# Layer 0: all three projections in one set of seven block products

## The chip, the cores and the metric

The kernel runs on one core of a Trainium2 chip. The metric is device time in microseconds (us) of one execution. The kernel before took 2167.6 us (median of three runs, 2166.02 to 2168.73). The profile is of one further execution.

The engines go by their profile names: PE (TensorE, matrix products), PEld (its weight loads), DVE (VectorE), ACT (ScalarE), POOL (GpSimd) and SP (SyncE, here only a queue that issues transfers). Lines such as L554 are lines of the kernel before; where a line of the changed kernel is meant, the text says so.

## The reference, cut to what matters

Two layers run on 4 x 512 tokens of width 512. Each layer adds an attention and a mixture of experts to its input. Only the attention of layer 0 is touched:

```python
xn = _layernorm(x)
q  = apply_rope(rmsnorm((xn @ Wq  + bq ).heads(16, 128), qn_w), pos)
lk = apply_rope(rmsnorm((xn @ Wlk + blk).heads(16, 128), kn_w), pos)
lv = (xn @ Wlv + blv).heads(16, 128)
ck = apply_rope(rmsnorm(entries @ Wk + bk, kn_w), block_ends)
cv = entries @ Wv + bv
ctx_sparse = top-8 attention of q over (ck, cv)
ctx_local  = windowed softmax attention of q over (lk, lv)
out = (0.5 * (ctx_sparse + ctx_local)) @ Wo + bo
```

`entries` are tokens averaged by fours with softmax weights. `rmsnorm` divides by the root of the mean square over the 128 elements of a head. `apply_rope` turns the first 64 of the 128 elements of a head and leaves the other 64 as they are. The scores of a query and a key are a sum over all 128 elements, so a factor on one of the 128 positions may sit on either side.

## The kernel before, in words

**Steps.** Layer 0 handles two heads (one group `g`) and one sequence of 512 tokens (`b`) at a time: 8 groups by 4 sequences are 32 steps. In step `i` the attention of step `i` is interleaved with the projections of step `i+1`; the projections of step 0 stand in the setup ahead of the loop. Other work (routing, experts, the sums of their results, the norm of the next layer) hangs on the places `run0((i, 0..4))` of each step. The two experts of a step are gathered, transposed (L382), multiplied (`apply`, L392: four products of 512 columns) and evicted by DVE (L394). A scheduler then orders the instructions of each engine. Each engine runs its own list in order.

**Projections.** A matmul takes 128 tokens as weights and streams the columns of a weight matrix, 256 for two heads. The queries are plain: for each half `t` of the sequence (256 tokens), `queries0(t)` does 2 x 4 matmuls of 256 columns into one PSUM bank (L554). Keys and values together use Winograd's form of Strassen's 2 x 2 block product: the tokens are cut into two halves, the width of 512 into two halves, and the columns into "keys" and "values"; seven block products `p1` to `p7` (L524) replace eight. Each is 2 x 2 matmuls of 256 columns into one bank. A step so has 16 + 28 = 44 matmuls of 256 columns. DVE forms sums of the input blocks (`sums_x`, L516 to L518, and L571), sums of the weights once per group (`combine_weights`, L102 to L106), and adds the products up as it evicts them (L561 to L587).

**After the projection.** `finish` and `rope` take the rows of two heads and two token blocks, four head rows of 128: ACT sums their squares (L432), POOL adds a constant and takes the power -0.5 (L434 to L437), DVE applies the rotation with tables `t1`, `t2` (L440 to L443), ACT scales the queries by the norm (L447). The keys stay unscaled; their norm enters as `scale` of the exponential (L613). Four PE transposes and one ACT copy (L543, L544) put a half of the queries or keys into `qkT`. The norm weights `qn_w` and `kn_w` are folded into the tables, which are 128 wide: cosine 1 in the unrotated half.

**Attention.** `scores(i, h)` does the sparse scores (L600), DVE's selection of eight (L603 to L625), the local scores (L609), exponentials (L613) and POOL's masks (L617). `turn` transposes the sparse weights (L635, L637), `context` multiplies with the values (L651 to L657), divides and adds the two halves (L660 to L670: ACT scales the sparse part into a tile `half`, DVE adds the local part). `turn_context` transposes (L677, L678), `output` multiplies with `Wo` (L685: eight products of 512 columns) and DVE adds to `acc` (L688).

**PSUM.** Layer 0 has 8 banks: 3 of tag "mm" (products, experts, output), 3 of "sc" (scores, context), 2 of "tr" (transposes). A bank is free again when DVE or ACT has read it.

**Setup.** SP issues the loads in the order x block 0, Wq, three bias broadcasts, x block 1, Wlk, the norm weights, cosine and sine tables, x blocks 2 and 3, Wlv, and the rest. `layernorm` (L199 to L211) runs on DVE, POOL (power), PE (transposes) and ACT (copy to `xnT`). `tables` (L176 to L195) builds the tables on POOL, ahead of the norms of blocks 2 and 3.

## Time and profile before

| what | value |
|---|---|
| median of three runs | 2167.6 us |
| the profiled execution | 2168.7 us, its span from first to last instruction 2166.8 us |
| PE busy | 2108.3 us, 97% of the span |
| DVE, ACT, POOL busy | 1458.9, 848.4, 687.0 us |
| granted PE clock, mean | 0.993 of full |
| PE idle in 0 to 54 us | 54.00 - 37.08 = 16.9 us |
| PE idle in 500 to 1000 us | 0.0 us |
| first sparse scores of step 0 | start at 61.16 us |
| a step between 520 and 990 us | 46.98 us (520.95, 567.93, 614.91 ... for the starts of L685) |

Busy time is the share in which an engine works on an instruction. PE's matmuls are pipelined: one of 256 columns has a duration of 0.38 us, but eight of them start and end within 3.46 us, 0.4325 us each. So costs on PE are taken from the starts in the order of time, not from the mean durations. Idle time is put down to what ended it.

### The profile page before, as it was taken

Reading aid. Unit: us, or ns where it says so; the run is one execution under the profiler, and the core shown is the slowest. Engines: PE = TensorE matmul, PEld = TensorE weight load, DVE = VectorE, ACT = ScalarE, POOL = GpSimd, SP = SyncE. Lnnn points to the kernel's source line nnn. Section 1 sums busy time; section 2 is a strip of 40 time slices with the busy share of each in tenths; the row PEclk is TensorE's granted clock in tenths of the full one; section 3 lists DMA queues with packets and bytes.
Section 4 is the critical chain, followed back from the end, with each engine's and each line's share of the span. In section 5 each row is a group of like instructions: output and inputs, shape, how many; then the busy total and the mean of one; then the engine's idle time right before and its main releaser. Section 6 shows DMA issues by size and latency. Waiting matters only on the chain.

```text
span 2166.8 us, 28936 instructions
## 1 busy us (share of the span) xinstructions
PE 2108.3 (97%) x9970; PEld 1392.0 (64%) x9970; DVE 1458.9 (67%) x3674; ACT 848.4 (39%) x2649; POOL 687.0 (32%) x725
## 2 busy tenths in 40 slices
PE   6999999999999999999999999999999999999998
PEld 5667877777777777777777887885334343443332
DVE  6868976666666766666666788885485444446775
ACT  3444444334444334444433444552333233333332
POOL 3212234343323323333323444443012222213430
PEclk9999999999999999999999999999999999999998
DMA  7001023322322332232232112102016566653321
GB/s 229 35 11 38 11 73 97 106 78 83 105 98 74 105 105 71 83 124 80 78 123 83 59 50 63 35 30 92 10 69 209 203 227 209 205 198 117 107 83 41
DMA packets 70813, 211.24 MB, mean 97 GB/s; under 512 B 8449, under 2 KB 25857, under 8 KB 60673
## 3 DMA queue, kind: packets, MB, share of 16 engines
q0 software_dynamic: 22592, 139.47, 19.2%
q1 hardware_dynamic: 45760, 65.63, 9.4%
q10 hardware_dynamic: 2304, 4.20, 0.5%
q8 instruction: 81, 1.33, 0.3%
q14 instruction: 76, 0.61, 0.1%
HBM read 176.24 MB, written 33.03 MB: 97 GB/s over the span
## 4 chain that ended last, share of the span: by engine, by line
PE 68%; issue 13%; DVE 8%; POOL 5%; DMA 3%; ACT 3%; SPq 0%; POOLq 0%; ACTq 0%; DVEq 0%
PE p L524 15%; PE pq L554 9%; PE op L685 9%; PE hp_r L392 7%; PE st L609 4%; PE sp L600 2%; PE trq L543 2%; PE qp L905 2%; POOL we_r L375 2%; PE ca L653 2%; PE o L976 1%; DVE pS L936 1%; PE st L916 1%; DMA row_r<-yd,slot_r 1%; PE cc L657 1%
## 5 line engine op out<-in xcount | busy, mean ns | idle before, releaser
L392 PE MATMUL hp_r<-we_r,xT_r 128*128 128x512 f32 x624 | 283.4, 597 | 4.3 <-DMA we_r<-in_ewx,wrow_r 4.2
L617 POOL TENSOR_TENSOR lT<-lT,lmask 128x512 f32<-128x512 f32 (+1 forms) x128 | 151.2, 1196 | 318.6 <-ACT lT L613 318.6
L554 PE MATMUL pq<-Wq,xnT 128*128 128x256 f32 x1024 | 234.0, 381 | 1.2 <-DVE u L570 1.2
L685 PE MATMUL op<-Wo,cT 128*128 128x512 f32 x512 | 230.5, 599 | 2.1 <-DVE lv L587 2.1
L554 PEld LDWEIGHTS pq<-Wq,xnT 128*128 128x128 f32 x1024 | 190.2, 191 | 24.9 <-DVE u L570 1.5
L392 PEld LDWEIGHTS hp_r<-we_r,xT_r 128*128 128x128 f32 x624 | 115.1, 191 | 139.4 <-issue 129.6
L373 POOL DMA_INDIRECT xr_r<-xnd,rows_r x78 | 83.6, 1072 | 330.9 <-PE trm_r L382 232.9
L613 ACT ACTIVATE lT<-st,ss 128x256 f32<-128x256 f32 (+1 forms) x256 | 96.8, 443 | 234.2 <-PE st L609 234.1
L544 ACT COPY qkT<-trq 128x512 f32<-128x512 f32 x128 | 74.7, 583 | 231.6 <-PE trq L543 231.2
L685 PEld LDWEIGHTS op<-Wo,cT 128*128 128x128 f32 x512 | 91.7, 190 | 113.8 <-issue 82.3
L918 ACT ACTIVATE pT<-st 128x1024 f32<-128x1024 f32 x128 | 123.8, 1019 | 70.1 <-PE st L916 54.5
L437 POOL TENSOR_TENSOR ss<-ss,nhalf 128x4 f32<-128x4 f32 x128 | 144.5, 1129 | 10.7
L384 ACT COPY xT_r<-trm_r 128x512 f32<-128x512 f32 x78 | 45.2, 580 | 260.6 <-PE trm_r L382 203.0
L688 DVE TENSOR_TENSOR acc<-acc,op 128x512 f32<-128x512 f32 x128 | 87.5, 684 | 80.7 <-PE op L685 80.5
L394 DVE TENSOR_TENSOR yr_r<-hp_r,we_r 128x512 f32<-128x512 f32 x78 | 53.7, 688 | 116.5 <-PE hp_r L392 116.5
L447 ACT ACTIVATE r<-r,ss 128x128 f32<-128x128 f32 x256 | 81.9, 390 | 105.8 <-POOL ss L437 103.4
L524 PE MATMUL p<-Wlv,x 128*128 128x256 f32 x512 | 117.5, 380 | 0.0
L524 PE MATMUL p<-Wlk,xnT 128*128 128x256 f32 x512 | 117.4, 383 | 0.0
L524 PE MATMUL p<-wT,x 128*128 128x256 f32 x512 | 117.4, 380 | 0.0
L407 POOL DMA_INDIRECT row_r<-yd,slot_r x64 | 75.3, 1176 | 120.1 <-DVE row_r L1008 53.6
L524 PEld LDWEIGHTS p<-wT,x 128*128 128x128 f32 x512 | 95.9, 190 | 23.8 <-issue 12.1
L524 PEld LDWEIGHTS p<-Wlv,x 128*128 128x128 f32 x512 | 95.5, 190 | 20.7 <-issue 9.1
(253 smaller groups left out, 4394.4 us busy)
## 6 DMA issues: line engine op xcount, KB each, us to landing
yd<-yr_r SPq DMA_DIRECT2D x78, 256.0 KB, 2.4
acc<-in_x SPq DMA_DIRECT2D x16, 256.0 KB, 5.1
Wq<-in_Wq SPq DMA_DIRECT2D x8, 512.0 KB, 3.7
Wlk<-in_Wlk SPq DMA_DIRECT2D x8, 512.0 KB, 3.6
xnd<-xn ACTq DMA_DIRECT2D x16, 256.0 KB, 2.6
Wlv<-in_Wlv SPq DMA_DIRECT2D x8, 512.0 KB, 9.1
Wo<-in_Wo SPq DMA_DIRECT2D x8, 512.0 KB, 3.6
xnd<-xn SPq DMA_DIRECT2D x16, 256.0 KB, 2.0
```

The lines of the kernel that those rows point to most:

```text
L373: G.indirect_dma_start(out=x, out_offset=None, in_=xnd, in_offset=at_rows(self.r.rows[:, i : i + 1]))
L392: PE.matmul(hp, lhsT=xT[:, k, :], rhs=w[:, ts(k, HID)], start=(k == 0), stop=(k == KC - 1))
L437: G.tensor_tensor(ss, ss, nhalf[:, 0:n], ALU.pow)
L447: A.activation(r1[:, h, :], r1[:, h, :], AF.Copy, scale=ss[:, h : h + 1])
L524: PE.matmul(p[:, c, :], lhsT=x[:, k, ts(c, P)], rhs=w[:, k, :], start=(k == 0), stop=(k == 1))
L554: PE.matmul(pq[:, c, :], lhsT=xnT[:, k, ds(b * S + (2 * t + c) * P, P)], rhs=w_q[:, k, :], start=(k == 0), stop=(k == KC - 1))
L609: PE.matmul(st[:, ds((t % 2) * 256, n)], lhsT=qkT[:, HG + h, ts(t, P)], rhs=qkT[:, h, ds(t * P, n)], start=True, stop=True)
L613: A.activation(lT[:, ds(half * 512 + c * 256, n)], st[:, ds(c * 256, n)], AF.Exp, scale=norm_k[(i, half)][:, c * HG + h : c * HG + h + 1])
L617: G.tensor_tensor(dst, dst, lmask.rearrange("p a w j -> p (a w j)")[:, 0:n], ALU.mult)
L685: PE.matmul(op, lhsT=cT[:, h, ts(t, P)], rhs=wo[:, h, :], start=(h == 0), stop=(h == HG - 1))
L688: V.tensor_tensor(acc[:, n, :], acc[:, n, :], op, ALU.add)
L918: A.activation(pt[:, ts(pair, 2), :], st, AF.Exp, scale=SCALE1)
```

## The change

It has these parts.

1. **Queries in the products.** The columns of a group are regrouped by the host into two matrices of 384: `wA` holds the two query heads and the key of head 0, `wB` the two value heads and the key of head 1. The seven products now run over these two column halves, 2 x 2 matmuls of 384 columns each, and yield queries, keys and values. The products of 16 matmuls for the queries (L554) are gone. A bank holds one token block: 14 evictions of 384 columns instead of 2 + 7 of 512.
2. **Sums of x.** They are formed only in the projections of steps 0 to 3 (now four sums, the fourth also at that place), written to a DRAM tile `xsd`, and loaded again for the same sequence in steps 4 to 31 (four loads of 256 KB each).
3. **Rotation.** Only the 64 rotated columns are touched, in place. The factor of the unrotated 64 positions is one column `turned`, applied by ACT as it copies the transposed keys. Squares run over six head rows (two query heads and one key head, two token blocks) and once over four (the second key head, inside `lv`).
4. **Order.** The products are spread: the first four ahead of the scores of head 1, `second(0)` and the query transposes ahead of the context of head 0, `second(1)` after it, `third` after the turn of head 1, `fourth`, the other query transposes, the keys of head 0 and `fifth` between the context of head 1 and the output. The keys of head 1 are transposed in the next step, after the scores of head 0. `qkT` has one buffer instead of two.
5. **Half sums in place.** ACT writes the sparse half into the context tile itself, and DVE adds to it there; the tile `half` is gone.
6. **Setup.** All four x blocks of the first sequence and the norm weights are loaded first, then `wA` and `wB` in two parts each with the tables between. The tables are 64 wide, and are built behind the first four norms. The norms of blocks 0 and 1 are kept in program order on DVE.

The diff, cut to its core:

```diff
-        for nm in ("Wq", "Wlk", "Wlv"):
-            w = wpool.tile([P, KC, HG * D], F32, tag=nm, name=f"{nm}_{g}")
+        for i, nm in enumerate(("wA", "wB")):
+            w = wpool.tile([P, KC, 3 * D], F32, tag=nm, name=f"{nm}_{g}")
...
-        t2_, t3_, t4_ = (wpool.tile([P, 2, HG * D], ...) for x in (2, 3, 4))
+        t2_, t3_, t4_ = (wpool.tile([P, 2, 3 * D], ...) for x in (2, 3, 4))
+        for o, x, y in ((t3_, b2_, b1), (b1, b1, w_a[:, 0:2, :]), (t2_, b2_, b1), (t4_, t2_, a2),
+                        (b2[:, 1, :], b2[:, 1, :], b2[:, 0, :])):
...
+    for n in range(TC):
+        load_x(n)
...
+    def load_sums(i):
+        for n in range(4):
+            xs[n] = wk0.tile([P, 2, 256], F32, tag=f"x{n}", name=f"x{n}_{i}", bufs=1)
+            if i >= B:
+                nc.sync.dma_start(out=xs[n].rearrange("p k t -> p (k t)"), in_=xsd[steps[i][1], n])
...
-        qkT = qp.tile([P, 2 * HG, S], F32, tag="qkT", name=f"qkT_{g}_{b}")
+        qkT = qp.tile([P, 2 * HG, S], F32, tag="qkT", name=f"qkT_{g}_{b}", bufs=1)
...
+        def product(nm, x, w, c):
+            p = psum("mm", f"{nm}_{i}_{c}")[:, 0 : 3 * D]
+            for k in range(2):
+                PE.matmul(p, lhsT=x[:, k, ts(c, P)], rhs=w[:, k, :], start=(k == 0), stop=(k == 1))
+            return p
...
+        def finish(t):
+            x = qb[t].rearrange("p c (h d) -> p (c h) d", d=D)
+            sq[t] = squares(x, 6, wk0, f"{i}_{t}", float(D))
+            by = lambda tt: tt[:, ts(t, 2), :, :].rearrange("p c h d -> p (c h) d")
+            rotate(x, by(t1), by(t2), 6, wk0, f"{i}_{t}")
+            for j in (0, 1, 3, 4):
+                A.activation(x[:, j, :], x[:, j, :], AF.Copy, scale=sq[t][:, j : j + 1])
...
+        def turn_keys(h):
+            tr = psum("tr", f"trk_{i}_{h}")
+            for t in range(TC):
+                PE.transpose(tr[:, ts(t, P)], lv[:, t, 2, 0:D] if h else qb[t // 2][:, t % 2, ts(2, D)], ident)
+            A.activation(qkT[:, HG + h, :], tr, AF.Copy, scale=turned[:, 0:1])
+        def first():
+        def second(c):
+        def third():
+        def fourth():
+        def fifth():
...
-            A.activation(half[:, t, :], spa[t][:, 0:D], AF.Copy, scale=sums[:, at : at + 1])
+            A.activation(ctx_[:, t, :], spa[t][:, 0:D], AF.Copy, scale=sums[:, at : at + 1])
...
         em0, lT0 = scores(i, 0, now)
+        turn_last(1)
+        if more:
+            load_sums(i + 1)
+            qkT, sums_x, first, second, third, fourth, fifth, turn_queries, turn_keys = project(i + 1)
+            first()
+            sums_x()
         run0((i, 0))
         em1, lT1 = scores(i, 1, now)
         sT0 = turn(i, 0, em0)
         run0((i, 1))
-        back_k1 = keys_b(back_q0)
-        back_k0()
+            second(0)
+            turn_queries(0)
         ctx0 = context(i, 0, lT0, sT0, lv)
+            second(1)
         sT1 = turn(i, 1, em1)
-        back_q1 = queries_b()
+            third()
         run0((i, 2))
-        back_k1()
         ctx1 = context(i, 1, lT1, sT1, lv)
         turn_context(i, 0, ctx0, cT)
         run0((i, 3))
-        values_()
-        back_q1()
+            fourth()
+            turn_queries(1)
+            turn_keys(0)
+            fifth()
         turn_context(i, 1, ctx1, cT)
         for t in range(TC):
             output(i, t, cT)
```

## The prediction

> **What bounds the kernel now.** First the page's busy times and slices, then the chain that ended last, then the costliest groups, and for prices one step in order of time.

> ```profile
> PE 2108.3 (97%) x9970; PEld 1392.0 (64%) x9970; DVE 1458.9 (67%) x3674; ACT 848.4 (39%) x2649; POOL 687.0 (32%) x725
> PE   6999999999999999999999999999999999999998
> ...
> PE 68%; issue 13%; DVE 8%; POOL 5%; DMA 3%; ACT 3%; SPq 0%; POOLq 0%; ACTq 0%; DVEq 0%
> ...
> L554 PE MATMUL pq<-Wq,xnT 128*128 128x256 f32 x1024 | 234.0, 381 | 1.2 <-DVE u L570 1.2
> ```

> PE is busy in every slice but the first and the last. L554, the queries' products, is 1024 matmuls (16 a step), with 1.2 us of idle before all of them. The stretches of busy time give 500.00 of 500 us for PE between 500 and 1000 us, and 37.08 of 54 at the start. So two things can pay: less PE work per step, and the 16.9 us of idle at the start. The prices on PE come from the order of time (start, duration of the merged piece, engine, line):

> ```profile
> 624.16 3.62 PE L554 MATMUL pq<-Wq,xnT 128*128 128x256 f32 x16
> 627.62 3.62 PE L524 MATMUL p<-Wlk,xnT 128*128 128x256 f32 x16
> ...
> 634.36 3.60 PE L392 MATMUL hp_r<-we_r,xT_r 128*128 128x512 f32 x8
> 637.79 3.62 PE L524 MATMUL p<-wT,x 128*128 128x256 f32 x16
> ```

> "x16" is 8 matmuls and 8 weight loads. From 624.16 to 627.62 eight matmuls of 256 columns take 3.46 us, 0.4325 each. The four of 512 (634.36 to 637.79) take 3.43, 0.857 each. The price follows the columns, not the count of matmuls: 384 lie in the middle, 0.645. The weight load (0.19) is hidden behind either.

> **PE work per step.** Before 44 x 0.4325 = 19.03 us, after 28 x 0.645 = 18.06: **-0.97**. The transposes stay at 16 of 128 rows, the attention is unchanged. The output's eight matmuls of 512 run in 7.00 us a step (614.75 to 621.75), 0.875 each; by that row 384 cost 0.654, and the gain is 19.03 - 18.31 = 0.72. I take 0.97, since the experts' and the small products agree with each other, and keep 0.72 as an end. 31 projections lie in the loop: 31 x 0.97 = **30 us**. If nothing but the count of matmuls mattered (28 x 0.4325) it would be 6.9 a step; the 512 row excludes that.

> **What must stay behind PE.** I went through a step in the order in which the changed program's instructions stand on each engine, PE back to back from T = 0 at the first sparse score: scores of head 0 to 2.4 us, keys of head 1 turned 2.85, `first` 8.0, expert turn and scores of head 1 10.85, turn 11.3, expert 14.7, `second(0)` 17.3, queries turned 17.7, context 0 20.2, `second(1)` 22.8, turn 23.2, `third` 25.8, expert turn 26.2, context 1 28.7, its first turn 29.1, expert 32.5, `fourth` 35.1, queries and keys turned 36.0, `fifth` 38.6, turn 39.0, output 46.0.

> DVE. Rows of before: 512 columns 0.69, 256 0.42, 128 0.28, so 384 are 0.555 and 768 0.96 (estimates from these). Before: 11 evictions and adds x 0.69 + 4 sums of x x 0.69 + 4 rotations x (0.70 + 2 x 0.283 + 0.42) = 17.1 us. After: 14 x 0.555 + 2 x 0.96 + 2 x (2 x 0.555 + 2 x 0.35) + (2 x 0.42 + 2 x 0.28) = 14.7. DVE has 2.4 us less in a step (about 0.4 less in steps 0 to 2, where the sums remain); it is 66% busy there, so this is cover, not gain. `combine_weights` grows by about 4 x 0.27 + 0.13 = 1.2 us in each of 8 groups, in the same cover. [...]

> The "mm" banks. Before, a bank holds 1.73 us of products; after, 1.29, so three banks cover 3.9 us of a DVE that looks away, not 5.2. Where DVE is away longest is head 0's selection (622.85 to 627.46, 4.6 us): it ends near T = 5.7, the first bank is wanted again at 6.7 and read by 6.2. The second tight place is `fifth`: its first bank (36.0) waits for the expert's eviction, which stands behind context 1's adds, which wait for ACT. There ACT has six squares (0.43 each between starts), POOL a power over six columns (1 column 0.59, 4 columns 1.13, so 1.49), ACT four scalings (1.2) and four of the context (1.0). Counted from the row block's eviction at 26.4 that makes the expert's eviction end at 34.5 to 35.0. The same chain of before, with four squares, took 651.1 to 657.8. Slack: 1.0 to 1.5 us. The queries' turn at 35.1 needs scalings that end near 31.6; slack 3.5.

> ACT at the end: the first square of key 1 stands ahead of the copy of context 1's turn, for which the output waits. It needs `fifth`'s first eviction (38.2); the copy can start at 39.1. Nothing if DVE is in time, up to 1 us if late. POOL has 3 powers for 4 (5.0 us a step for 5.8, each with its constant of 0.31). ACT's half sums in place change no count.

> DMA. The x sums are 1 MB a step more (28 steps), on engines 28% busy between 500 and 1000 us. A buffer comes free at T = 22.8 to 38.6 of the step before, the data is wanted at 14.7 to 36.0; x loads of this size landed in 5.1 us. In SP's order they stand behind the experts' stores of the step before, which have gone by then. Free; if the cover went, 5 us a step.

> `qkT` in one buffer: the first write waits for scores that PE did 6 us earlier. Nothing. Steps 24 to 30: PE idles 0.4 to 1.3 us a step for context adds or `lv` (0.44 and 0.89 around 1261 and 1267); DVE is lighter, but in step 26 five sums of weights fall between context 1's sums and its adds. Together +-6; I take **+1**.

> **Setup.** The waits of PE in the first 500 us:

> ```profile
> PE trx L210 <- DVE xn L206: 11.3, 1, 11.3
> ...
> PE trx L210 <- DVE mv L203: 3.3, 1, 3.3
> PE lg_r L219 <- ACT xnT L211: 2.1, 1, 2.1
> ```

> Block 0 of x is there at 3.56 us, block 1 at 9.73, blocks 2 and 3 at 16.4 and 18.3; the tables occupy POOL from 15.58 to 20.6, ahead of the powers of norms 2 and 3; so `p6` starts at 33.64. After, four blocks (1 MB) go first; all norms end before the tables. What then decides is the weights: by 22.9 us before, 3.55 MB had landed (155 GB/s). bA ends at 2.5 MB, wB at 3.3: by that rate 16 and 21 us, by the best slices (390 GB/s, from 2 us on) 8 and 10. Then `first`, six squares, tables (4.7 us on POOL for 3 x (256 + 2 x 128 columns), from 1.58 for 640 and 0.57 for 160), power, scalings, and on DVE four sums of weights: `p6` at 25.6 to 27.8 instead of 33.64. Of these 6 to 8 us, 0.8 goes back, since more products lie behind that point (20 x 0.645 = 12.9 against 28 x 0.4325 = 12.1). From there on DVE is full in both kernels. I take **-7**; ends 0 (wB no earlier than Wlv was) and -13.

> [...]

> **Sum.** -30 - 7 + 1 = -36.5 on the profiled execution's 2168.7 us (span 2166.8 and 1.9 around it): 2132. The median of the runs lies 1.1 lower: **2131 us**.

> **Rivals.**
> (a) *The gain is part lost.* Products cost by the output row (-0.72: 31 x 0.25 = 8 us less), or the two slacks of 1 us fail in part, 0.3 us in 31 steps = 9, or wB is late, 7. One or two of these: 2139 to 2155. For it: the smaller banks and the ACT square ahead of the copy; against it: the ledger.
> (b) *More gain.* The start loses 13, the stalls of steps 24 to 30 vanish (6): 2131 - 12 = 2119, at most 2113.
> (c) *Slower.* The queries' and keys' turns now stand in PE's queue between `fourth` and `fifth`, 8.7 us after the eviction of their rows (26.4 to 35.1); the last queries of before had 9.8 (651.1 to 660.9) and one chain less to share ACT with. If squares, power and scalings take 3.5 us longer than my ledger, every step waits; from 3.5 + 1.2 = 4.7 us on the gain is gone, and at 6 us the price is 31 x 2.5 = 78 against 36: 2173 or more. For it: one engine's power feeds all. Against: the chain of before is known, 6.7 us, and 2 squares and 2 columns add 1.2.
> (d) *It doesn't do what it says:* some other stall of 1.2 us a step eats it all, 2163 to 2172.

> **How the numbers follow.** Forecast (2119 to 2139) 0.58; (a) 0.24; (b) 0.09; (c) 0.05; (d) 0.04. No change is within 0.2%, 4.3 us, which is what a measurement of this kernel can tell. Faster 0.58 + 0.24 + 0.09 = 0.91, same 0.04, slower 0.05. The range 2115 to 2150 takes in both ends of the setup, the 0.72 row, and most of (a) and (b).

> **What would show it.** A step between 500 and 1000 us: 46.0 us, PE still 500 of 500, eight matmuls of 384 in 5.16. If 7 us are gone at the start, the first sparse scores come at 53 to 55 us instead of 61.16. Rows "PE p3 or p5 <- DVE" or "op <- ACT cT" of over 10 us in PE's waits mean (a), "trq <- ACT" means (c). Wrong outright: a step of 46.98 or more.

## The result, and the profile after

The changed kernel takes **2175.26 us** (median of 20 runs, 2168.43 to 2181.54) against 2169.70 us (20 runs, 2166.02 to 2174.88): ratio **1.0026**, 95% interval 1.0018 to 1.0034. It is slower by a quarter of a per cent, where I had forecast 2131 us. The profiled execution took 2178.08 us (span 2176.3); that of before 2168.7 (span 2166.8).

From the page of the changed kernel (engine, busy time, share of the span, instructions; the span in 40 slices; the chain that ended last):

```profile
PE 2091.1 (96%) x8946; PEld 1202.5 (55%) x8946; DVE 1454.5 (67%) x3596; ACT 868.7 (40%) x2649; POOL 686.0 (32%) x667
...
PE   7999999999999999999999999898999999999997
...
PE 68%; issue 10%; DVE 9%; POOL 5%; DMA 4%; ACT 3%; SPq 0%; POOLq 0%; ACTq 0%; DVEq 0%
```

There are 1024 matmuls fewer, but TensorE is busy for only 17.2 us less (2108.3 before), and there are now two slices of 8 past the middle of the span, where before had none. To find the place I took the time at which the output product of each step starts, in both traces, and compared the stretches between them:

| stretch | before, us | after, us | difference | forecast |
|---|---|---|---|---|
| start to output of step 0 | 100.23 | 99.29 | -0.94 | -8 |
| outputs of steps 0 to 7 | 326.60 | 326.00 | -0.60 | -6.8 |
| 7 to 23 (steady) | 751.67 | 735.92 | -15.75 | -15.5 |
| 23 to 30 | 289.03 | 311.81 | **+22.78** | -5.8 |
| 30 to 31 | 24.30 | 24.85 | +0.55 | 0 |
| 31 to the end (layer 1) | 675.0 | 678.4 | +3.4 | 0 |

The forecast column is the record's own terms: 0.97 for each projection, 7 for the start (the start holds one projection too), +1 for steps 24 to 30. (They add up to -36; the -36.5 on record is a slip of half a microsecond.) The steady steps do exactly what the ledger said: 45.99 us a step (46.98 before), TensorE busy 500.00 of 500 us. The order of time of TensorE in the changed kernel shows the new price:

```profile
573.07 5.33 PE L538 MATMUL p<-wA,xnT 128*128 128x384 f32 x16
578.23 0.60 PE L392 MATMUL trm_r<-ident,xr_r 128*128 128x128 f32 x4
```

Eight matmuls of 384 columns in 5.16 us, 0.645 each. So the loss is not in the change's own arithmetic. It is in steps 24 to 30, where no expert product is left and the rows of the experts are gathered and added instead, and in the start.

**Steps 24 to 28.** VectorE's waits in that stretch, for the rows of the experts (in total, times, longest), of the changed kernel and then of before:

```profile
DVE acc L712 <- DMA row_r<-yd,slot_r: 17.6, 12, 3.3
```

```profile
DVE acc L695 <- DMA row_r<-yd,slot_r: 1.3, 5, 0.4
```

One case in order of time, VectorE, GpSimd and TensorE of the changed kernel (start, duration, engine, line, operation; in brackets the idle time ahead of it and what ended it):

```profile
1268.40 0.75 DVE L712 SCALAR_TENSOR_TENSOR acc<-row_r,gate_r,acc 128x512 f32<-128x512 f32 x1
1269.42 0.74 DVE L712 SCALAR_TENSOR_TENSOR acc<-row_r,gate_r,acc 128x512 f32<-128x512 f32 x1
...
1275.88 0.75 DVE L712 SCALAR_TENSOR_TENSOR acc<-row_r,gate_r,acc 128x512 f32<-128x512 f32 x1 [2.41 <-DMA row_r<-yd,slot_r]
...
1277.47 0.75 DVE L712 SCALAR_TENSOR_TENSOR acc<-row_r,gate_r,acc 128x512 f32<-128x512 f32 x1 [0.77 <-DMA row_r<-yd,slot_r]
...
1280.39 0.55 DVE L577 TENSOR_TENSOR u<-p,u 128x384 f32<-128x384 f32 x1
```

```profile
1269.64 2.63 POOL L635 TENSOR_TENSOR lT<-lT,lmask 128x512 f32<-128x512 f32 x2
1272.43 1.15 POOL L417 DMA_INDIRECT row_r<-yd,slot_r  x1 [0.16 <-issue]
1273.88 0.95 POOL L417 DMA_INDIRECT row_r<-yd,slot_r  x1 [0.30 <-issue]
```

```profile
1276.68 1.46 PE L538 MATMUL p<-wT,xnT 128*128 128x384 f32 x4
1280.99 2.93 PE L538 MATMUL p<-wT,xnT 128*128 128x384 f32 x4 [2.85 <-DVE u L577]
```

Read it from the top. The row buffers come free at 1269.15 and 1270.16. The next gathers stand on GpSimd behind two masks, are issued at 1272.43 and 1273.88, and their rows land about 3.5 us after issue (the median of both kernels). VectorE arrives at the next add at 1273.47, 1.0 us after the issue, waits 2.41 and 0.77 us, and then has the context's sums before it reaches the evictions of `second(1)` at 1280.39: for 7.3 us it has left the banks alone. TensorE has filled its three "mm" banks meanwhile and idles 2.85 us. In the kernel before, the same gathers (those of the second place of step 26) had far more time:

```profile
1268.64 0.75 DVE L695 SCALAR_TENSOR_TENSOR acc<-row_r,gate_r,acc 128x512 f32<-128x512 f32 x1
...
1269.90 0.75 DVE L695 SCALAR_TENSOR_TENSOR acc<-row_r,gate_r,acc 128x512 f32<-128x512 f32 x1
...
1285.63 0.75 DVE L695 SCALAR_TENSOR_TENSOR acc<-row_r,gate_r,acc 128x512 f32<-128x512 f32 x1
```

```profile
1269.66 0.94 POOL L407 DMA_INDIRECT row_r<-yd,slot_r  x1 [3.83 <-DVE acc L695]
1270.92 0.95 POOL L407 DMA_INDIRECT row_r<-yd,slot_r  x1 [0.32 <-DVE acc L695]
```

There the first place's adds (1268.64 and 1269.90) stood ahead of head 0's selection, and GpSimd issued the next gathers as soon as the buffers were free. The selection and the evictions and rotations of queries and keys lay between them and the next adds: issue to use took 16.0 us. In the changed order the first place's adds have moved behind the selection and `first`'s evictions (1268.40), and only `second(0)` and a part of the next selection stand between them and the second place's adds. Over steps 25 to 28 VectorE comes to the second place's adds 1.0, 1.1, 0.2 and 1.1 us after the issue, where it came after 16.0, 16.0, 12.6 and 16.0.

After the idle time comes the clock. Windows of the changed kernel, the columns being the length, busy time of PE, PEld, DVE, ACT and POOL, and then the granted clock:

```profile
1280.00:1288.00 8.00, 7.01 (x29) 5.80 (x30) 5.50 (x14) 2.78 (x14) 1.92 (x2) 0.57 0.11 33
```

0.57 over 8 us is 6.8 us at half clock. Between the outputs of steps 23 and 30 half clock lasts 13.7 us (before: none), which is 6.8 us of work lost; TensorE's idle time there is 25.2 us against 4.3. Together 27.7 of the 28.6 us by which that stretch missed its forecast (22.8 + 5.8).

**The start.** `p6` starts at 31.38 instead of 33.64, not at 25.6 to 27.8. Of the changed kernel, VectorE, GpSimd, TensorE:

```profile
13.23 0.55 DVE L216 TENSOR_SCALAR xn<-acc,mv 128x512 f32<-128x512 f32 x1 [3.18 <-DMA xnd<-xn]
```

```profile
19.11 0.73 POOL L192 TENSOR_TENSOR t<-cs,nw 128x256 f32<-128x256 f32 x1 [8.37 <-DVE nw L189]
...
27.11 1.56 POOL L444 TENSOR_TENSOR ss<-ss,nhalf 128x6 f32<-128x6 f32 x1
```

```profile
29.15 0.48 PE L558 MATMUL trq<-ident,qb 128*128 128x128 f32 x1 [3.43 <-ACT qb L552]
...
31.38 6.87 PE L538 MATMUL p<-wT,x 128*128 128x384 f32 x16 [0.35 <-DVE wT L104]
```

The tile of norm rows, xn, has two buffers, and the third norm waits 3.18 us for a store of the first one to leave. Everything behind it on VectorE comes late: the scaling of the norm weights, the tables, the first power, the turn of the queries (3.43 us idle on TensorE), and half clock from 27.5 to 34.3 us (granted 0.59 in the mean of 26 to 34).

### The profile page after: what moved, and what is told of

It is laid out like the page before. It is cut to its first block, busy times and chain, and to the rows that moved or that the text cites. A ratio compares the mean times of both kernels' runs of the same rounds, so it can differ in the third digit from the quotient of the medians.

```text
span 2176.3 us, 27397 instructions
## 1 busy us (share of the span) xinstructions
PE 2091.1 (96%) x8946; PEld 1202.5 (55%) x8946; DVE 1454.5 (67%) x3596; ACT 868.7 (40%) x2649; POOL 686.0 (32%) x667
## 4 chain that ended last, share of the span: by engine, by line
PE 68%; issue 10%; DVE 9%; POOL 5%; DMA 4%; ACT 3%; SPq 0%; POOLq 0%; ACTq 0%; DVEq 0%
PE p L538 21%; PE op L702 10%; PE hp_r L402 8%; PE st L627 3%; PE qp L934 3%; PE sp L618 2%; PE st L945 2%; DMA row_r<-yd,slot_r 2%; PE o L1005 2%; PE ca L671 1%; PE cx L959 1%; PE vp L924 1%; ACT sq L442 1%; PE trk L564 1%; PE po L1055 1%
## 5 line engine op out<-in xcount | busy, mean ns | idle before, releaser
L538 PE MATMUL p<-wT,x 128*128 128x384 f32 x512 | 180.1, 493 | 2.9 <-DVE u L577 2.6
L538 PE MATMUL p<-wB,x 128*128 128x384 f32 x512 | 179.2, 491 | 0.8 <-DVE yr_r L404 0.7
L538 PE MATMUL p<-wA,xnT 128*128 128x384 f32 x512 | 173.2, 491 | 3.9 <-DMA wA<-in_wA 3.9
L442 ACT ACTIVATE sq<-qb 128x128 f32<-128x128 f32 x384 | 119.0, 310 | 93.0 <-DVE qb L584 51.3
L705 DVE TENSOR_TENSOR acc<-acc,op 128x512 f32<-128x512 f32 x128 | 87.5, 684 | 68.2 <-PE op L702 67.9
L538 PEld LDWEIGHTS p<-wA,xnT 128*128 128x128 f32 x512 | 95.4, 192 | 63.7 <-issue 5.1
L538 PEld LDWEIGHTS p<-wB,x 128*128 128x128 f32 x512 | 93.9, 192 | 60.9 <-issue 10.8
L552 ACT ACTIVATE qb<-qb,ss 128x128 f32<-128x128 f32 x256 | 81.9, 389 | 111.9 <-POOL ss L444 99.6
L631 ACT ACTIVATE lT<-st,ss 128x256 f32<-128x256 f32 (+1 forms) x128 | 46.9, 449 | 190.1 <-PE st L627 190.1
L627 PE MATMUL st<-qkT 128*128 128x256 f32 (+1 forms) x512 | 108.4, 353 | 0.0
L538 PE MATMUL p<-wT,xnT 128*128 128x384 f32 x256 | 93.6, 506 | 9.7 <-DVE u L577 9.7
```

The source lines that it names most:

```text
L442: A.activation(sq, x[:, h, :], AF.Square, accum_out=ss[:, h : h + 1])
L538: PE.matmul(p, lhsT=x[:, k, ts(c, P)], rhs=w[:, k, :], start=(k == 0), stop=(k == 1))
L552: A.activation(x[:, j, :], x[:, j, :], AF.Copy, scale=sq[t][:, j : j + 1])
L627: PE.matmul(st[:, ds((t % 2) * 256, n)], lhsT=qkT[:, HG + h, ts(t, P)], rhs=qkT[:, h, ds(t * P, n)], start=True, stop=True)
L705: V.tensor_tensor(acc[:, n, :], acc[:, n, :], op, ALU.add)
```

## The experiments

Theory A is that in steps 24 to 28 the adds stand on VectorE ahead of evictions that TensorE needs, and wait there for gathers that cannot be issued earlier. Rival B is that the new order is too slow there without any gather, rival C that the clock, or the reloaded sums of x, do it by themselves. For each kernel the table gives the sum of steps 24 to 28 and of steps 29 and 30 between output starts, from one profile each, and the median time; the labels are those of the runs below.

| kernel | steps 24-28 | 29 and 30 | median, us |
|---|---|---|---|
| before | 206.98 | 82.05 | 2169.7 |
| changed | 223.32 | 88.49 | 2175.3 |
| b_nocomb | 200.83 | 82.11 | 2165.3 |
| a_nocomb | 201.51 | 88.10 | 2156.9 |
| a_place1 | 218.48 | 87.40 | 2265.9 |
| a_two_places | 200.99 | 91.38 | 2161.8 |
| a_two_late | 201.00 | 92.24 | 2161.9 |
| a_direct | 201.96 | 88.33 | 2158.1 |
| d_adds | 202.32 | 88.34 | 2146.7 |
| best | 202.25 | 86.34 | 2144.4 |

**Without the gathers and adds**, in the changed kernel and in before:

```diff
-    for n in range(NT):
-        jobs0.append((at[n], lambda n=n: rout.__setitem__(n, combine(rout["ex"], n))))
-        jobs0.append((at[n + 1], lambda n=n: rout.pop(n)()))
```

> The changed kernel without the 32 gathers of expert rows of layer 0 and the 32 adds that take them into acc (L415-L418 and L705-L712 are not called; layer 0 lacks its expert terms). Theory A (the adds stand on VectorE ahead of the evictions and wait there for gathers issued just before, so TensorE lacks a bank, idles 2.7 to 3.3 us, and its clock is halved after that): steps 24 to 28 lose these idles and the half-clock stretches; a step there costs the steady 46.0 us less two experts of about 3.9 us, so 38 to 39 us instead of 43 to 48, and the whole comes to 2140 to 2148 us. Rival B (the ScalarE and GpSimd chain of the new order is too slow in a step with no expert work; the gathers are innocent): steps 24 to 28 stay at 41 us or more, the whole at 2160 or more. Rival C (the reloads of the x sums collide with the gathers, or the clock falls for reasons of its own): half-clock stretches remain in 1200 to 1400 us.

> The kernel before without the same gathers and adds. Theory A: the adds cost little here, since the gathers are issued 8 to 11 us ahead of them; steps 24 to 28 go from 40.4-43.1 to the steady 46.98 less two experts, 39 to 40 us, and the whole falls by 5 to 10 us, to 2160 to 2165 us: so the pair without gathers differs by 17 to 25 us in favour of the change. Rival B: the pair differs by less than 5 us or the change is still the slower one. Rival C: as theory A for this kernel alone.

a_nocomb: 2156.85 us, ratio to before 0.9941 (0.9924 to 0.9957). b_nocomb: 2165.28, 0.9980 (0.9968 to 0.9992). The adds cost the changed kernel 21.8 us in steps 24 to 28 (223.32 to 201.51) and before 6.2. No half clock is left in steps 24 to 28; the one stretch between 1200 and 1400 us, 3.4 us from 1384.8, lies in step 29, behind a wait for a norm. So C falls as the cause of these steps (its other half, reloads that slow the gathers, too: gathers land 3.5 us after issue in both kernels). The rest was missed. Steps 25 to 28 take 38.8 to 40.1 us where I expected 38 to 39, the whole is 2156.85 and not 2140 to 2148, and b_nocomb lies just above its range. The pair differs by 8.4 us and not by 17 to 25: without gathers both kernels need the same 201 us, so the 0.97 us a step is missing here also without them. TensorE's waits in a_nocomb between 1140 and 1500 us say why:

```profile
PE trk L564 <- ACT cT L695: 3.9, 4, 1.0
PE trx L220 <- DVE xn L216: 2.4, 1, 2.4
```

In four of these five steps the turn of head 0's keys waits 1.0 us for a "tr" bank, until ScalarE has copied the turned context of head 0 out of it; b_nocomb's list does not have such a row. In order of time in step 25, ScalarE and TensorE:

```profile
1236.78 1.28 ACT L552 ACTIVATE qb<-qb,ss 128x128 f32<-128x128 f32 x4 [2.09 <-POOL ss L444]
...
1238.96 0.59 ACT L695 COPY cT<-trc 128x512 f32<-128x512 f32 x1
```

```profile
1239.60 0.66 PE L564 MATMUL trk<-ident,qb 128*128 128x128 f32 x4 [0.96 <-ACT cT L695]
```

ScalarE is late because it has itself waited 2.09 us for GpSimd's power over six columns, and then does the scalings and the context first. And the wait for a norm of layer 1 (second row) is there without any gather: steps 29 and 30 have a cause of their own.

**The work of the second place moved back**, one line:

```diff
-        run0((i, 1))
         if more:
             second(0)
...
             third()
+        run0((i, 1))
```

> The changed kernel with the work of the second place of a step (expert product, or gather and add) moved behind context 0, second(1), head 1's turn and third: one line moved. The gathers of that place then have some 8 us more and the adds stand behind the evictions of second(1) and third. Theory A: TensorE's idles on the eviction L577 in 1160-1470 us go, and with them most of the 13.6 us of half clock there; steps 24 to 28 come to 40 to 43 us, the whole to 2150 to 2165 us. Steps 5 to 23 stay at 46.0, or rise if the expert's product is badly placed there. Rivals B and C: steps 24 to 28 stay at 43 to 48, the whole at 2170 to 2180.

2265.85 us, ratio 1.0450 (1.0432 to 1.0469): a miss, and an edit that changed too much to decide between the theories. The place serves the experts' products too, and steps 5 to 23 went from 46.0 to 50.8 us in the mean, where TensorE now waits, among others, for the weights of the next expert, which have one buffer. And in steps 24 to 28 the adds, now ahead of `fourth` and `fifth`, mostly moved TensorE's wait to the output (VectorE's waits for row_r still add up to 13.0 us, 17.6 in the changed kernel):

```profile
694.36 3.70 PE L402 MATMUL hp_r<-we_r,xT_r 128*128 128x512 f32 x8 [1.65 <-DMA we_r<-in_Wex,wrow_r]
```

```profile
1303.98 8.11 PE L702 MATMUL op<-Wo,cT 128*128 128x512 f32 x12 [3.68 <-DVE lv L599]
```

**Half as many adds in a step, gathered two places or one place ahead:**

```diff
+    at.append((len(steps) - 1, 4))
+    to = [min(2 * n, 14 + n) + 1 for n in range(NT)]
     for n in range(NT):
-        jobs0.append((at[n], lambda n=n: rout.__setitem__(n, combine(rout["ex"], n))))
-        jobs0.append((at[n + 1], lambda n=n: rout.pop(n)()))
+        jobs0.append((at[to[n - 1] if n else 0], lambda n=n: rout.__setitem__(n, combine(rout["ex"], n))))
+        jobs0.append((at[to[n]], lambda n=n: rout.pop(n)()))
```

(a_two_late asks for the gather at `at[to[n] - 1]`.)

> The changed kernel with the combination spread over twice the steps: one add of a block of 128 tokens at every second place, and its gather issued two places ahead of it, right behind the add before. Theory A: no add waits for its gather any more (row_r waits of VectorE under 3 us in all, 17.6 now), steps 24 to 30 come to 39 to 41 us without half clock, the whole to 2145 to 2155 us. Rival B: the steps stay at 43 or more although the waits for row_r are gone. Rival C: half-clock stretches remain, at other places.

> The changed kernel with the adds at the same places as in the run that spread them over twice the steps, but each gather only one place ahead of its add instead of two: the same number of adds per step, a shorter distance. Theory A (the distance from gather to add is the cause): row_r waits of VectorE of 8 us or more return, TensorE idles on evictions behind the adds at the second place, half clock comes back in 1160-1470 us, and the whole is 2165 to 2175 us. Rival (the density of adds on VectorE is the cause, the distance is not): steps 24 to 28 stay at 38 to 40.5 us and the whole at 2160 to 2164.

a_two_places: 2161.78 us, 0.9967 (0.9955 to 0.9978). No wait for row_r, no half clock in 24 to 28, 200.99 us as without gathers: theory A's numbers for those steps, and the whole misses its range because steps 29 to 31 got longer (91.4 and 28.4 us). a_two_late: 2161.88 us, 0.9968 (0.9956 to 0.9979), with the same steps: this was the rival's number. But it did not do what it was made for. In its trace GpSimd and VectorE show

```profile
1202.46 1.05 POOL L417 DMA_INDIRECT row_r<-yd,slot_r  x1 [3.92 <-DVE acc L712]
```

```profile
1201.44 0.74 DVE L712 SCALAR_TENSOR_TENSOR acc<-row_r,gate_r,acc 128x512 f32<-128x512 f32 x1
...
1226.41 0.74 DVE L712 SCALAR_TENSOR_TENSOR acc<-row_r,gate_r,acc 128x512 f32<-128x512 f32 x1
```

The scheduler had issued the gather as soon as the add before had freed the buffer, 24 us ahead of its use, wherever the program asked for it. So density and distance were still one thing: with one buffer for each row, one add per place means a short distance.

**The same density, the rows brought another way:**

```diff
-                G.indirect_dma_start(out=x, out_offset=None, in_=self.yd,
-                                     in_offset=at_rows(self.r.slot[:, k, n : n + 1]))
+                if self.silu:
+                    G.indirect_dma_start(out=x, out_offset=None, in_=self.yd,
+                                         in_offset=at_rows(self.r.slot[:, k, n : n + 1]))
+                else:
+                    nc.sync.dma_start(out=x, in_=self.yd[ts(2 * n + k, P), :])
```

> The changed kernel with the 32 gathers of expert rows of layer 0 replaced by 32 plain loads of the same size from the same array, issued by SyncE instead of GpSimd (each takes 128 rows in order, so layer 0 adds wrong rows); one add at every place, one buffer for each row, as in the changed kernel. Theory A (the gather is late because it stands on GpSimd behind the add before it and behind two masks, 3.2 us): the loads are issued about 3 us earlier, VectorE's waits for row_r fall from 17.6 to under 6 us, steps 24 to 28 take 39 to 41.5 us, and the whole is 2155 to 2164 us. Rival (the density of one add per place is the cause, whatever brings the rows): the steps stay at 43 to 48, the whole at 2170 or more.

2158.14 us, 0.9957 (0.9942 to 0.9973); steps 24 to 28 take 43.3, 39.0, 41.6, 38.5 and 39.6 us. VectorE's list of waits has no row for row_r any more, no half clock is left in layer 0 behind 285 us. VectorE and SyncE:

```profile
1222.89 0.74 DVE L715 SCALAR_TENSOR_TENSOR acc<-row_r,gate_r,acc 128x512 f32<-128x512 f32 x1
...
1223.91 0.74 DVE L715 SCALAR_TENSOR_TENSOR acc<-row_r,gate_r,acc 128x512 f32<-128x512 f32 x1
...
1227.89 0.74 DVE L715 SCALAR_TENSOR_TENSOR acc<-row_r,gate_r,acc 128x512 f32<-128x512 f32 x1
...
1228.67 0.75 DVE L715 SCALAR_TENSOR_TENSOR acc<-row_r,gate_r,acc 128x512 f32<-128x512 f32 x1
```

```profile
1223.66 6.11 SPq L421 DMA_DIRECT2D row_r<-yd  x4
```

The adds follow each other even more closely than in the changed kernel (1223.91 to 1227.89), and none waits: SyncE issues the load the moment the buffer is free (1222.89 + 0.74), GpSimd did so 3.3 us later. So it is not the number of adds. It is the late issue of the gather, which stands in GpSimd's queue behind the masks, with one buffer for each row. (Two loads whose landing the trace shows took 2.7 us, against 3.5 for a gather.) Theory A holds: steps 24 to 28 take 21.4 us less than in the changed kernel, which is what leaving the adds out altogether gave (201.96 and 201.51), and the median is 17.1 us lower. Which of the two would be enough by itself, a second buffer for each row or the gathers ahead of the masks on GpSimd, no run here shows.

**The start, the marks, the norms.** The next kernels have edits in separate stretches, so that each is read by itself. All carry the routing marks one place later in step 4, the adds at every second of five places (the place behind the output counts too), and the turn of a norm's rows one place behind the norm. c_xn has three buffers for xn; c_early instead the order `tables, combine_weights, sums_x, first`; c_all both, and the first turn of the queries behind `third`.

```diff
-        xn = pool.tile([P, HID], F32, tag="xn", name=f"xn_{n}")
+        xn = pool.tile([P, HID], F32, tag="xn", name=f"xn_{n}", **({"bufs": 3} if pool is sp0 else {}))
...
-    for b, place in enumerate(((3, 4), (4, 0), (4, 1), (4, 2), (4, 3))):
+    for b, place in enumerate(((3, 4), (4, 0), (4, 2), (4, 3), (4, 4))):
...
+    fives = [(i, h) for i in range(24, len(steps)) for h in range(5)]
+    to = [fives[3 + 2 * n] for n in range(NT)]
```

In c_xn, c_early, c_all and d_norms the last four blocks of the norm of layer 1 are never turned: the closure that puts the turn off is not called for them. So 16 transposes and four copies of layer 1 are left out (about 2 us of TensorE at the 0.11 us of a transpose), and their whole time is not a like-for-like figure; the stretches of layer 0 are.

> The changed kernel with four edits in separate stretches, each read by itself from the starts of the output products. (1) Start: three buffers for the norm rows xn instead of two, so that the third norm does not wait 3.18 us for a store. (2) Step 4: the routing marks one place later, off the place ahead of second(0). (3) Steps 24 to 30: an add of expert rows at every second of five places (behind the output too), its gather issued two places ahead; the last one in step 30. (4) Steps 29 to 31: the rows of a norm of layer 1 are turned on TensorE one place after VectorE wrote them. Theory A: (1) the norm scaling, and with it the tables and the first power, come 3 us earlier, the first output product at 95 to 97 us instead of 99.29; (2) step 4 in 43.7 to 44.5 us instead of 46.50, without half clock; (3) steps 24 to 28 in 38 to 40.5 us; (4) the steps that end as numbers 29 and 30 come from 46.3 and 42.2 to 41 and 40.5; the whole to 2135 to 2145 us. Rival for the start (the weights' landing and VectorE's order set p6 anyway): the first output product stays at 98 to 99.3. Rival for 24 to 30 (the new order itself is slow without expert work): (3) stays over 41 us.

> As the run before in its edits (2) to (4), but at the start the order is changed instead of the buffers: the sums of the first weights and of x stand on VectorE ahead of first's evictions and rotation, the tables ahead of both. Theory A (p6 waits for wT, which VectorE makes only behind the rotation, which waits for the tables on GpSimd): p6 starts at 22 to 25 us instead of 31.4, the first output product at 92 to 95. If wB's landing decided it: p6 not before 28, the output at 97 or later. The turn of the queries may still wait for its scalings, with half clock behind it: then 95 to 97.

> All of it: the three xn buffers, the early sums, and besides the first turn of the queries behind third's products, so that TensorE does not wait for tables, power and scalings at 25.7 to 29.2; with edits (2) to (4). Theory A: no TensorE idle over 2 us between 16 and 60 us and no half clock there, the first output product at 89 to 93 us (the forecast's setup term was 7 us less than 100.2), the whole 2128 to 2140 us, faster than both kernels. Rival: VectorE is full from 20 us on, and what TensorE gains at p6 it gives back before the first scores: the output product at 96 or later, the whole 2138 to 2148.

| kernel | p6, us | first scores | output of step 0 | steps 0 to 4 | whole, us |
|---|---|---|---|---|---|
| before | 33.64 | 61.16 | 100.23 | 185.08 | 2169.7 |
| changed | 31.38 | 63.71 | 99.29 | 186.58 | 2175.3 |
| c_xn | 27.19 | 58.62 | 93.20 | 183.33 | 2142.68 (one run) |
| c_early | 24.27 | 58.92 | 98.78 | 184.60 | 2148.81 (one run) |
| c_all | 24.51 | 56.80 | 93.12 | 184.80 | 2142.78, 0.9870 (0.9850 to 0.9891) |

One buffer more is worth 6.1 us at the output of step 0, and with it the start is 7.0 us under before, the term of the forecast. (That it comes out at just 7.0 is partly luck. In the profiles of kernels with two buffers and otherwise the changed kernel's start that output comes at 98.4 to 101.3 us, with three at 92.7 to 94.2.) In c_xn the tables start at 14.12 instead of 19.11 us, and the queries' turn follows the logits' without a wait:

```profile
14.12 0.73 POOL L192 TENSOR_TENSOR t<-cs,nw 128x256 f32<-128x256 f32 x1 [3.80 <-DMA wB<-in_wB]
```

```profile
25.63 0.41 PE L241 MATMUL trg_r<-ident,lr_r 9*128 9x9 f32 x4 [3.74 <-ACT lr_r L236]
25.98 0.66 PE L563 MATMUL trq<-ident,qb 128*128 128x128 f32 x4
26.56 0.63 PE L467 MATMUL wt<-ident,lr_r 1*128 1x1 f32 x4
27.19 7.12 PE L543 MATMUL p<-wT,x 128*128 128x384 f32 x16
```

TensorE still idles 3.74 us here, for a copy of ScalarE that stands behind the scalings of the queries, and half clock still follows from 27.2 us on (6.96 us for eight matmuls of 384 columns, 5.16 at full clock): the same chain holds it, some 4 us earlier. The fourth norm still waits 3.07 us for a store; four buffers were not tried. The three kernels take 202.3 to 202.5 us for steps 24 to 28, in single steps of 37.4 to 43.4 where 38 to 40.5 was expected.

c_early got its `p6` at 24.27, as expected, but the output at 98.78, four to seven microseconds later than expected: an early `p6` alone buys nothing. It lost the lead again to the rotation behind late tables (2.12 us on TensorE at 31), to the compressed keys, and to half clock at 92 us (two matmuls of 384 columns in 2.56 us from 91.97, 1.29 at full clock). c_all shows the same: p6 at 24.51, output at 93.12 (89 to 93 expected), no better than c_xn; the whole, 2142.78, is over its 2128 to 2140. So the xn buffer decides, not the order. Step 4 went from 46.50 to 44.53 with the marks moved, about 2 of the 2.8 us it had lost (43.68 before). Putting off the turns of the norms did nothing for steps 29 and 30 (46.99 and 43.23 us); so the next two kernels leave that out, or put the norm itself one place earlier:

```diff
+        i, t = 29 + n // TC, n % TC
+        jobs0.append(((i, t - 1) if t else (i - 1, 4), lambda n=n: next_layer(n, rout["pool"], psum)))
+        jobs0.append(((i, t), lambda n=n: rout.pop(("turn", n))()))
```

> The changed kernel with the three xn buffers at the start, the routing marks one place later, and the adds at every second of five places; the norms of layer 1 as in the changed kernel. Against the run with the norms' turns put off as well this shows what that edit does by itself. Theory A: first output product at 93.2 us, steps 24 to 28 at 37.5 to 41.7, and the two steps with norms (ends 29 and 30) at 45 to 47 and 42 to 43 as in the changed kernel: the adds have nothing to do with them. Whole 2138 to 2145 us. If the put-off turns had been what made those steps long, they come to 41 each and the whole to 2134.

> As the run beside it, but the norms of layer 1 one place earlier (the first of a sequence right behind the last output product, as the kernel before has them on VectorE by its order: xn at 1392 us, ahead of the scores' selection), their turns at the old place, and the adds at three of five places, none ahead of the first norm. Theory A (steps 29 and 30 wait 3.6 us for a norm that stands behind selection, adds and a power behind two masks and two gathers): TensorE's wait on xn is under 1 us, the two steps take 41 to 42.5 us, the whole 2132 to 2138. Rival (those steps are bound by ScalarE's chain or by VectorE's sum of work): they stay at 43 to 47.

d_adds: 2146.72 us, 0.9896 (0.9878 to 0.9914), a little over its range; steps 29 and 30 at 45.8 and 42.5, as in the changed kernel. a_nocomb has the same length of them without any add, so the adds are not their cause. d_norms: 2146.84, 0.9890 (0.9869 to 0.9912), the two steps at 48.4 and 42.4, no better; theory A's number for them failed. In both, VectorE and TensorE wait in the norm itself. Of d_adds, between 1340 and 1480 us:

```profile
DVE xn L216 <- POOL mv L214: 2.5, 1, 2.5
```

```profile
PE trx L220 <- DVE xn L216: 3.6, 1, 3.6
```

VectorE stands 2.5 us in line for a power on GpSimd, which is behind other work in GpSimd's queue: two gathers in d_adds, a gather and masks in d_norms (there 2.7 us, and evictions come 1.64 us late by it), two masks in a_nocomb and in the changed kernel. So the last kernel puts a place between the statistics with their power, the rows, and their turn; the adds are at three of five places.

```diff
+    to = [(24, 4)] + [(i, h) for i in range(25, 29) for h in (0, 2, 4)] + [(29, 2), (29, 4), (30, 2)]
...
+        jobs0.append(((i, t - 1) if t else (i - 1, 4), lambda n=n: begin_norm(n)))
+        jobs0.append(((i, t), lambda n=n: norm_rows(n)))
+        jobs0.append(((i, t + 1), lambda n=n: norm[n][1]()))
```

> The changed kernel with the three xn buffers, the routing marks one place later, adds of expert rows at three of five places with their gathers right behind the add before, and the norms of layer 1 in three places: statistics and power first, the rows one place later, their turns on TensorE one more place later. Theory A (VectorE stood 2.5 us in a norm for a power on GpSimd behind masks and gathers, and TensorE in line behind it): no wait of VectorE for that power over 1 us and of TensorE for xn over 1 us, the steps that end as 29 and 30 at 41 to 43 us (45.8 and 42.5 without it), layer 0 done at 1462 us or earlier, the whole 2134 to 2142 us by the state of the clock in layer 1. Rival (ScalarE's chain or VectorE's sum bounds those steps): 44 and more, no gain over the run without it.

**2144.41 us, 0.9896 (0.9876 to 0.9916)**: faster than both kernels, 31 us under the changed one, though above the 2134 to 2142 expected. VectorE's wait for the power is down to 0.5 us, TensorE's for the norm's rows is gone from the list, and steps 29 and 30 take 42.5 and 43.8 us: the first as expected, the second a little over, and the last output starts at 1464.6, not by 1462. Against d_adds the two steps are 2.0 us shorter; the medians (four runs each) cannot tell the two kernels apart.

## Why the prediction was wrong, point by point

- **PE work per step, -30.** Right in mechanism and size for the steady steps: 0.645 per matmul, 45.99 us a step, -15.75 us over 16 of them. The lower end (0.72) is excluded. Right too: the x loads are free, and TensorE stays at 500 of 500 us. The cover beside it did not come: evictions of 384 columns took the 0.55 us estimated, but VectorE did not get 2.4 us a step lighter. It is busy 31.0 us a step between 500 and 1000 us (30.9 before), since among others the L642 operation of the selection takes 1.35 us now where its like, L624, took 0.84. In the steady steps that cost nothing.
- **Steps 24 to 30, "Together +-6; I take +1".** This is the step that failed. I had gone through VectorE's order for a steady step and had counted the adds of the last steps as load (VectorE is lighter there), not as instructions that can wait. I had not put the gathers into GpSimd's queue, nor asked how much VectorE work would stand between one add and the next once the first place's adds had moved behind `first`. VectorE came 1.0 us after the issue instead of 16.0, with 3.5 needed. The cover of 3.9 us by the smaller "mm" banks, which I had priced against a VectorE that looks away for a selection, was what gave way. The adds cost 21.8 us instead of 6.2, and the sum had that at nothing. Of the 28.6 us by which this stretch missed, the 15.7 between these two are the largest part; the gain missing in steps 24 to 28 without any gather is 5.5, and steps 29 and 30 without any gather (a_nocomb against before) are 6.0 longer instead of 1.9 shorter.
- **The second tight place, "Slack: 1.0 to 1.5 us".** This chain (six squares, power, scalings, the context, ACT's copy) holds in steps with an expert's product, where there was no such wait. In steps 24 to 28, which have none, it is late once the gathers are out of the way: the keys' turn waits 1.0 us in each of four steps (a_nocomb, a_two_places), 3.9 of the 5.5 us of gain missing there. The copy for which the output waits, "up to 1 us if late", is another one.
- **The norms in steps 29 and 30** were not in my ledger at all: 88.5 us against 82.05. One part is the norm's power in GpSimd's queue: with the norm taken apart the two steps are 86.3. The rest is open.
- **Setup, -7.** It was 0.9. I had checked when the weights land, and they did not limit it. I had not counted the buffers of xn: four norms in a row with two buffers wait for a store. With a third buffer it is 7.0, and `p6` comes at 27.19, inside the 25.6 to 27.8 of the sum. (The tables' 4.7 us in it is a slip: its own two rows, 1.58 and 0.57, make 5.3, and c_xn has 5.5.) My marker, first scores at 53 to 55 us, was wrong even then (58.62): from `p6` to the scores it takes 31.4 us and not the 27.5 of before, from the scores to the output 34.6 and not 39.1, so more of step 0's work now stands ahead of the scores.
- **Steps 0 to 7**: forecast -6.8, measured -0.6. Step 4 took 2.8 us more instead of 1 less, for the marks ahead of an eviction (2.56 us idle, then half clock); 2 us of this are shown by moving the marks. The other 2.4 us I have not taken apart.
- **Rivals.** (c) put the slower outcome into the queries' and keys' turns of every step; "trq <- ACT" is 5.6 us in all between 1140 and 1500 us, and nothing in the steady steps. Nearest was (d), "some other stall eats it all", which I gave 0.04 without looking for a stall that lies outside the steady step; 2175 is over even its 2163 to 2172. The signs that I named looked at the start and at the steady step, and none at steps 24 to 30.
- **Layer 1**, 3.4 us more: it takes 671.5 to 681.3 us in the profiles of the kernels above that leave nothing of it out, with the half-clock stretches in different places. I read nothing from it.

## What to carry to other kernels

A ledger of a steady step says nothing of the stages in which other work takes its slots: do it once for each kind of step, with everything that sits in an in-order queue. When work is spread, ask for every DMA with a single buffer what now stands between the release of the buffer and the next use, on the issuing engine too. A stall of 3 us on TensorE then can cost more than itself, since half clock can follow: the 2.85 us idle from 1278.14 in the changed kernel came with 6.8 us at half clock, 3.4 us of work.

## What the runs showed of the hardware

**One table on GpSimd took 6.97 us while VectorE was busy.** In c_early the first table on GpSimd took ten times what the others of its shape took:

```profile
18.81 6.97 POOL L192 TENSOR_TENSOR t<-cs,nw 128x256 f32<-128x256 f32 x1 [9.18 <-DMA acc<-in_x]
...
26.56 0.73 POOL L192 TENSOR_TENSOR t<-cs,nw 128x256 f32<-128x256 f32 x1
```

From 18.76 to 25.1 us VectorE ran nine adds and subtractions back to back, the early sums of weights and of x. What held the table, and whether these sums had to do with it, no run shows. (In c_all, with the same order, the tables' operations took 0.72 to 1.44 us.)
